# Batched self-attention with batch norm: which engine adds up three pairs of output groups, when segment rows are scaled, and the order of stores and loads in one queue

## The chip, the cores and the metric

The kernel runs on one core of a Trainium2 chip. The metric is the time of one execution on the device in microseconds; lower is better. The time of the kernel before is the median of three runs.

## The reference

There are 16384 tokens with 256 features (fp32), and each token belongs to one of 8 segments. Attention runs within a segment, over at most 3072 positions; a batch norm over all tokens follows, then a ReLU and a residual:

```python
q, k, v = feat @ Wq, feat @ Wk, feat @ Wv
starts = jnp.searchsorted(bids, jnp.arange(B))
pos = jnp.arange(N) - starts[bids]
qp, kp, vp = pad(q), pad(k), pad(v)          # zeros(B, 3072, .).at[bids, pos].set(x)
attn = softmax(where(mask, einsum('bld,bmd->blm', qp, kp), -1e9))
r = einsum('blm,bmd->bld', attn, vp)[bids, pos]
t = r @ Wt
tn = (t - t.mean(0)) / sqrt(t.var(0) + EPS) * gamma + beta
return feat + relu(tn)
```

The segment numbers are not sorted in these inputs. So most tokens have a position outside the 3072 places of their segment; their result is that of the segment's first or last place, one of 16 "edge rows". Only some 400 to 730 tokens of each segment own a place.

## The kernel before, in words

The function `fast_path` writes instructions for five engines through a small recorder (`pg`). Each engine carries out its instructions in the order in which they were recorded; the recorder puts in a semaphore wait wherever an operand asks for one. TensorE is PE, VectorE DVE, ScalarE ACT, GpSimd POOL; SP issues plain DMAs and computes nothing. SP's DMAs go through one queue, GpSimd's indirect DMAs through another, and both are carried by the same 16 DMA engines.

First come the attention of the eight segments, the sums for the batch norm, and the factors of the norm: these end at `y3` (line 1868), the normed edge rows after the ReLU in three bf16 parts. The change lies behind that, in the output stage (lines 1882 to 1949).

Three things are done there.

**Most tokens.** The tokens are cut into 16 groups of 1024 (1 MB each way), taken in the order `ORDER` (line 1056) and handled two at a time, as "pairs" `c` = 0 to 7 (lines 1897 to 1925). The features of a group are loaded by SP into one of nine buffers `fb` (`f0` to `f8`; `group_in`, line 1670), so load 9 reuses the buffer of group 0 and has to wait until store 0 has landed. Each group has four units of 128 x 512. For each, PE multiplies a one-hot matrix with `y3` into a PSUM bank. Then there are two ways to add the features:

- VectorE adds the bank to the unit in place (`pg.tt`, recorded at line 826), or
- PE also multiplies the unit by the identity into the same bank (line 1904), and ACT copies the bank over the unit (line 822).

`by_act` (line 1900) chooses: in pairs 1 to 7 ACT takes the units x = 4 and 6, VectorE x = 0 and 2. Seven PSUM banks are used in turn, so the eighth tile of a pair takes the bank of its first.

**Stores.** When a group's units are done SP issues its store (line 1920). Behind it stands, for groups from the third on, `finish` of the group two places earlier: SP waits for that store's landing and counts it in the semaphore `done` (line 1893). Then come loads for later groups, by the table `LATER`.

**Tokens that own a place.** Their rows lie in `tk`, up to six tiles of 128 rows for a segment. `rows(e)` (line 1882) scales, shifts, clips and adds the features on VectorE: two passes at line 826 that read the factors from PSUM, one at line 846 that reads two SBUF tiles. One segment is done after each pair. Rows that lose a place to another token (`tl`) are done last, by `normal` (line 1932). GpSimd then scatters the tiles into the output, one indirect DMA of 128 rows (131 KB) each (line 1939). These must overwrite what the plain stores wrote, so ahead of segment `e` GpSimd waits until `done` has reached the last group that the segment's tokens touch (line 1935). With these inputs the counts waited for are 3, 5, 5, 7, 7, 7, 11, 11 landings for segments 0 to 7, the tiles 4, 4, 5, 6, 6, 6, 4, 4; the closing `tl` scatters need 11 landings too.

Of the kernel before, what the change touches and what calls it, by code (L numbers as in the profile page):

```python
# [29 lines left out]
LT = 3  # L30
# [869 lines left out]
def fast_path(nc, feat, bids, wq, wk, wv, wt, gamma, beta, out, bad):  # L900
# [23 lines left out]
    def new(name, shape, dtype=F32):  # L924
        nonlocal end
        size = mybir.dt.size(dtype)
        for d in shape[1:]:
            size *= d
        plan.append((name, shape, dtype, end))
        h = at(name, shape, dtype, end)  # L930
        end += size + -size % 32
        return h
# [32 lines left out]
    xl, tl = new("xl", [P, LT, D]), new("tl", [P, LT, D])  # L965
# [253 lines left out]
    def present(e, t):  # L1219
        return ExitStack() if t < 4 else pg.given(e, t - 4)  # L1220
# [449 lines left out]
    def group_in(i, after=()):  # L1670
        pg.dma("SP", fb[i % NF][:], feat3[ORDER[i]], after)
# [108 lines left out]
    e = NB - 1  # L1780
# [58 lines left out]
    def unit(i, x):  # L1839
        return fb[i % NF][:, x : x + 2, :].rearrange("p t d -> p (t d)")  # L1840
# [29 lines left out]
    def normal(parts):  # L1870
        def over_t(s_, T):
            return norm[:, s_ * D : (s_ + 1) * D].unsqueeze(1).to_broadcast([P, T, D])

        for step in range(3):
            for when, y, x, T in parts:
                with when():
                    if step < 2:
                        pg.tt(y, y, over_t(step, T), (ALU.mult, ALU.add)[step])
                    else:
                        pg.stt(y, y, 0.0, x, ALU.max, ALU.add)  # L1880

    def rows(e):
        m = e * FT
        parts = [
            ((lambda lo=lo: present(e, lo)), tk[:, m + lo : m + hi, :], xs[:, m + lo : m + hi, :], hi - lo)
            for lo, hi in ((4, 5), (5, 6), (0, 4))
        ]
        normal(parts)
# [3 lines left out]
    def finish(w):  # L1892
        pg.op("SP", lambda e: e.sem_inc(done, 1), [], [], after=[w])  # L1893

    LATER = {5: (9, 10), 6: (11, 12), 7: (13,), 8: (14,), 9: (15,)}
    stores = []
    for c in range(NG // 2):
        pair = (2 * c, 2 * c + 1)
        for x in range(0, GT, 2):
            by_act = x >= 4 if c else x in (2, 4)  # L1900
            pf = [bank[(c * GT + x + r) % 7] for r in range(2)]
            if by_act and c:
                for r, i in enumerate(pair):
                    pg.mm(pf[r][:], ident[:], unit(i, x), start=True, stop=False)
            for u in range(2):
                for r, i in enumerate(pair):
                    h = slice(64 * r, 64 * r + 6 * NB)
                    pg.mm(
                        pf[r][:, u * D : (u + 1) * D], hot[h, c, x + u, :], y3[h, :],
                        start=not by_act, stop=True,  # L1910
                    )
            for r, i in enumerate(pair):
                if by_act:
                    pg.copy("ACT", unit(i, x), pf[r][:])
                else:
                    pg.tt(unit(i, x), unit(i, x), pf[r][:], ALU.add)
        for i in pair:
            f = fb[i % NF]
            stores.append(
                pg.op("SP", lambda e, i=i, f=f: e.dma_start(out3[ORDER[i]], f[:]), [f[:]], [], dma=True)  # L1920
            )
            if i >= 2:
                finish(stores[i - 2])
                for k_ in LATER.get(i, ()):
                    group_in(k_)
        rows(c)
        if c == 0:
            pg.ts(good[:], rdens[:], LIM, ALU.is_lt)
            pg.stt(good[:], rdens[:], 1.0 / LIM, good[:], ALU.is_gt, ALU.mult, accum=odd[:])
            pg.ts(odd[:], odd[:], -1.0, ALU.mult, float(TT), ALU.add)  # L1930
            pg.red(cnt_f[:, 0:1], over[:])
    normal([(ExitStack, tl[:], xl[:], LT)])

    for e in range(NB):
        pg.op("POOL", lambda x, e=e: (x.wait_ge(done, 1), x.wait_ge(done, pg.regs[("POOL", ("g", e))])), [], [])
# [30 lines left out]
def whole(nc, feat, bids, wq, wk, wv, wt, gamma, beta, out):  # L1966
    with nc.sbuf_tensor("bad", [P, 1], I32) as bad:
        regs, marks = fast_path(nc, feat, bids, wq, wk, wv, wt, gamma, beta, out, bad)
        engines = {"PE": nc.tensor, "ACT": nc.scalar, "DVE": nc.vector, "POOL": nc.gpsimd, "SP": nc.sync}
        for name, eng in engines.items():  # L1970
            eng.br_lt(regs[(name, "bad")], 1, on_true="all_done", on_false="any_lengths").branch_hint(marks[name])
        with nc.body("any_lengths", valid_engines=tuple(mybir.ALL_ENGINES)):
            nc.all_engine_barrier()
            with tile.TileContext(nc) as tc:
                any_lengths(tc, feat, bids, wq, wk, wv, wt, gamma, beta, out)
            nc.br("all_done")
        nc.switch_bb("all_done")
# [34 lines left out]
```

## Time and profile before

| | |
|---|---|
| median of three runs | 315.19 us (313.87 to 315.64) |
| profiled execution, its own time | 314.44 us |
| its span in the profile | 312.1 us |
| first store issued | 232.72 us |
| last scatter issued | 308.11 us |
| VectorE busy over the span | 225.7 us (72%) |
| PE, ACT, GpSimd busy | 252.1, 139.2, 126.8 us |
| DMA packets, mean rate | 56.84 MB, 182 GB/s |

The profile is one execution; times in it are microseconds from the start of the span. The engines' rows give start, duration, engine, line, operation, output<-inputs, sizes, how many were merged into the row ("x4"), and in brackets the idle time ahead of it with what ended it. A line is often that of a helper (826 is any addition of two tensors on VectorE), so the tiles' names tell more. SPq is SP issuing; a DMA takes longer than its issue, until it has landed.

### The profile page before, as it was taken

How to read it: one execution, taken by the hardware profiler on the slowest of the kernel's cores; microseconds unless marked ns; L12 is line 12 of the kernel's file. 1: busy time of each engine (PE TensorE's matmuls, PEld its weight loads, DVE VectorE, ACT ScalarE, POOL GpSimd, SP SyncE). 2: the span in 40 equal slices, each digit the busy share in tenths (PEclk: the TensorE clock that was granted, in tenths of full speed). 3: DMA queues.
4: the chain of work that ended last, by engine and by line, in shares of the span. 5: the costliest groups of instructions: out<-in, count | busy, mean ns of one | idle time of the engine just before them, and what ended most of it. 6: DMA issues, size and time to landing. Idle time of an engine off the chain costs nothing.

```text
span 312.1 us, 4505 instructions
## 1 busy us (share of the span) xinstructions
PE 252.1 (81%) x1206; PEld 168.3 (54%) x1206; DVE 225.7 (72%) x712; ACT 139.2 (45%) x298; POOL 126.8 (41%) x155
## 2 busy tenths in 40 slices
PE   1789788898798898999999999989977947675510
PEld 1656666665675777687878778757532212212100
DVE  7866778889979896736664765766389999794550
ACT  7345334367464628644754583574422311212110
POOL 3436580430430071006313753742221257677275
PEclk9998897999799999999999999999999995979585
DMA  3102069522222021112031330679997899999995
GB/s 98 35 24 64 6 200 345 174 68 70 67 67 70 34 70 29 67 61 81 26 95 36 90 101 17 196 274 377 326 391 322 355 351 404 424 417 413 420 417 204
DMA packets 23241, 56.84 MB, mean 182 GB/s; under 512 B 4768, under 2 KB 15858, under 8 KB 19114
## 3 DMA queue, kind: packets, MB, share of 16 engines
q1 hardware_dynamic: 17434, 45.77, 39.5%
q0 software_dynamic: 5232, 10.18, 10.1%
q10 hardware_dynamic: 544, 0.52, 0.5%
q8 instruction: 14, 0.23, 0.3%
q14 instruction: 17, 0.14, 0.1%
HBM read 26.73 MB, written 28.61 MB: 177 GB/s over the span
## 4 chain that ended last, share of the span: by engine, by line
PE 42%; DVE 26%; DMA 16%; ACT 7%; issue 6%; POOL 1%; POOLq 0%; DVEq 0%; SPq 0%; ACTq 0%
PE ps L807 39%; DMA out<-f 12%; DVE acc L846 4%; DMA f<-in_r_feat 4%; PE ps L812 2%; DVE junk L833 2%; DVE w L826 2%; DVE k L823 2%; ACT pa L817 1%; POOL out L892 1%; DVE ge L835 1%; DVE both L851 1%; ACT pb L817 1%; ACT sq L817 1%; ACT tk L817 1%
## 5 line engine op out<-in xcount | busy, mean ns | idle before, releaser
L882 POOL DMA_INDIRECT xs<-in_r_feat,idx x48 | 51.3, 1068 | 101.0 <-DVE idx L846 76.9
L807 PE MATMUL ps<-vs,pa 128*128 128x257 f32 x312 | 74.9, 389 | 4.7 <-ACT sq L817 3.6
L807 PEld LDWEIGHTS ps<-vs,pa 128*128 128x128 f32 x312 | 58.1, 193 | 16.8 <-ACT sq L817 4.8
L807 PE MATMUL ps<-f,ident 128*128 128x512 f32 x64 | 39.7, 733 | 20.1 <-DMA f<-in_r_feat 16.1
L892 POOL DMA_INDIRECT out<-tk,idx x39 | 40.0, 1027 | 31.3 <-SPq L1893 20.9
L817 ACT ACTIVATE tk<-ps,rdens 128x256 f32<-128x256 f32 x46 | 22.2, 483 | 62.5 <-DVE rdens L859 62.4
L822 ACT COPY f<-ps 128x512 f32<-128x512 f32 x32 | 17.1, 590 | 55.3 <-PE ps L807 55.3
L807 PE MATMUL ps<-wvt,xT 128*128 128x256 f32 x156 | 38.9, 400 | 0.3 <-DVE acc L846 0.3
L807 PEld LDWEIGHTS ps<-wvt,xT 128*128 128x128 f32 x156 | 30.6, 200 | 10.6 <-issue 4.1
L807 PEld LDWEIGHTS ps<-f,ident 128*128 128x128 f32 x64 | 12.2, 221 | 35.8 <-DMA f<-in_r_feat 19.6
L846 DVE SCALAR_TENSOR_TENSOR acc<-sq,reads_r,acc 128x256 f32<-128x256 f32 x45 | 21.6, 480 | 8.8 <-ACT sq L817 8.8
L826 DVE TENSOR_TENSOR f<-f,ps 128x512 f32<-128x512 f32 x32 | 20.1, 682 | 10.6 <-DMA f<-in_r_feat 10.0
L817 ACT ACTIVATE pa<-ps,mask 128x512 f32<-128x512 f32 x39 | 24.0, 690 | 7.5 <-PE ps L807 7.4
L826 DVE TENSOR_TENSOR tk<-tk,ps 128x1024 f32<-128x1024 f32 (+1 forms) x30 | 24.2, 843 | 0.3
L882 POOL DMA_INDIRECT reads_r<-reads_of,idx x12 | 13.4, 1119 | 24.8 <-ACT sq L817 11.8
L846 DVE SCALAR_TENSOR_TENSOR acc<-tk,reads_r,acc 128x256 f32<-128x256 f32 x45 | 21.5, 477 | 1.2 <-ACT tk L817 0.7
L807 PE MATMUL ps<-q,k 32*128 32x512 f32 (+2 forms) x154 | 20.6, 478 | 1.5 <-ACT pa L817 1.1
L823 DVE COPY k<-ps 32x128 f32<-32x128 f32 x40 | 11.8, 294 | 13.5 <-PE ps L807 12.6
L807 PE MATMUL ps<-xT,w 128*128 128x512 f32 (+1 forms) x60 | 20.6, 476 | 0.6 <-ACT xT L817 0.5
L807 PE MATMUL ps<-vs,pb 128*128 128x257 f32 x82 | 19.6, 387 | 0.0
L807 PEld LDWEIGHTS ps<-vs,pb 128*128 128x128 f32 x82 | 15.1, 189 | 6.5 <-issue 2.3
L817 ACT ACTIVATE q<-ps,cqk 96x512 f32<-96x512 f32 (+3 forms) x24 | 14.6, 608 | 7.8 <-PE ps L807 7.6
(260 smaller groups left out, 356.2 us busy)
## 6 DMA issues: line engine op xcount, KB each, us to landing
f<-in_r_feat SPq DMA_DIRECT2D x16, 1024.0 KB, 13.1
out<-f SPq DMA_DIRECT2D x16, 1024.0 KB, 10.1
t_rows<-tk SPq DMA_DIRECT2D x8, 512.0 KB, 3.9
xs<-zt SPq DMA_DIRECT2D x5, 768.0 KB, 10.4
t_rows<-tk SPq DMA_DIRECT2D x8, 256.0 KB, 2.5
eb<-edge_of SPq DMA_DIRECT2D x16, 96.0 KB, 2.3
xs<-in_r_feat,idx POOLq DMA_INDIRECT x48, 2.8
out<-tk,idx POOLq DMA_INDIRECT x39, 7.2
```

Of the source, the lines that this page charges most:

```text
L807: "PE", lambda e: e.matmul(out, lhsT, rhs, start=start, stop=stop, skip_group_check=True),
L812: return self.op("PE", lambda e: e.transpose(out, in_, ident), [in_, ident], [out])
L817: "ACT", lambda e: e.activation(out, in_, func, bias=bias, scale=scale), [in_, *more], [out]
L822: return self.op("ACT", lambda e: e.copy(out, in_), [in_], [out])
L823: return self.op(eng, lambda e: e.tensor_copy(out, in_), [in_], [out])
L826: return self.op(eng, lambda e: e.tensor_tensor(out, a, b, op), [a, b], [out])
L833: lambda e: e.tensor_scalar(out, a, s1, s2, op0, op1, accum_out=accum)
L835: else e.tensor_scalar(out, a, s1, s2, op0, op1),
L846: else e.scalar_tensor_tensor(out, a, s, b, op0, op1),
L851: return self.op("DVE", lambda e: e.tensor_reduce(out, in_, AX.X, op), [in_], [out])
L882: lambda e: e.indirect_dma_start(out=out, out_offset=None, in_=table, in_offset=bass.IndirectOffsetOnAxis(ap=ind, axis=0), bounds_check=n ...
L892: lambda e: e.indirect_dma_start(out=table, out_offset=bass.IndirectOffsetOnAxis(ap=ind, axis=0), in_=src, in_offset=None, bounds_check=n ...
```

## The change

Five things are changed, all in the output stage:

- In pairs 1 to 3 ACT takes only x = 6, and VectorE adds three units of each group instead of two.
- The rows of segments 0 to 3 are scaled one pair later, those of 4 and 5 after pair 5, those of 6 and 7 after pair 6.
- Both stores of a pair are issued first, and only then does SP wait for the landings of the pair before.
- The loads 9 to 12 come singly, one behind each counted landing.
- The `tl` rows are scaled ahead of pair 7 instead of last, and four short instructions on counts stand after pair 3 instead of pair 0.

```diff
-    LATER = {5: (9, 10), 6: (11, 12), 7: (13,), 8: (14,), 9: (15,)}
+    LATER = {3: (9,), 4: (10,), 5: (11,), 6: (12,), 7: (13,), 8: (14,), 9: (15,)}
+    ROWS = {1: (0,), 2: (1,), 3: (2,), 4: (3,), 5: (4, 5), 6: (6, 7)}
     stores = []
     for c in range(NG // 2):
         pair = (2 * c, 2 * c + 1)
         for x in range(0, GT, 2):
-            by_act = x >= 4 if c else x in (2, 4)
+            by_act = x >= (6 if c < 4 else 4) if c else x in (2, 4)
...
             stores.append(
                 pg.op("SP", lambda e, i=i, f=f: e.dma_start(out3[ORDER[i]], f[:]), [f[:]], [], dma=True)
             )
+        for i in pair:
             if i >= 2:
                 finish(stores[i - 2])
                 for k_ in LATER.get(i, ()):
                     group_in(k_)
-        rows(c)
-        if c == 0:
+        for e in ROWS.get(c, ()):
+            rows(e)
+        if c == 6:
+            normal([(ExitStack, tl[:], xl[:], LT)])
+        if c == 3:
             pg.ts(good[:], rdens[:], LIM, ALU.is_lt)
...
-    normal([(ExitStack, tl[:], xl[:], LT)])
```

SP's rows show what this does to its queue. Each row is an instruction; `out_0<-f3_79` is the store of the buffer `f3`, `f0_76<-in_r_feat` a load into `f0`, and in brackets stand the semaphores waited for: `of_SP_22` to `of_SP_25` are the landings of stores 0 to 3, `at_DVE` and `at_ACT` the engines that fill the buffer. Before, from the third store to the seventh:

```order
L1920 DMA out_0<-f2_78 128x2048 [waits at_DVE,at_ACT,of_SP_12]
L1920 DMA out_0<-f3_79 128x2048 [waits of_SP_22,at_DVE,at_ACT]
L1920 DMA out_0<-f4_80 128x2048 [waits of_SP_23,at_DVE,at_ACT,of_SP_15]
L1920 DMA out_0<-f5_81 128x2048 [waits of_SP_24,at_DVE,at_ACT]
L877 DMA f0_76<-in_r_feat 128x2048 [waits of_SP_25]
L877 DMA f1_77<-in_r_feat 128x2048
L1920 DMA out_0<-f6_82 128x2048 [waits at_DVE,at_ACT,of_SP_17]
```

The same place in the changed kernel:

```order
L1921 DMA out_0<-f2_78 128x2048 [waits at_DVE,at_ACT,of_SP_12]
L1921 DMA out_0<-f3_79 128x2048 [waits at_DVE,at_ACT]
L877 DMA f0_76<-in_r_feat 128x2048 [waits of_SP_22,of_SP_23]
L1921 DMA out_0<-f4_80 128x2048 [waits at_DVE,at_ACT,of_SP_15]
L1921 DMA out_0<-f5_81 128x2048 [waits at_DVE,at_ACT]
L877 DMA f1_77<-in_r_feat 128x2048 [waits of_SP_24]
L877 DMA f2_78<-in_r_feat 128x2048 [waits of_SP_25]
L1921 DMA out_0<-f6_82 128x2048 [waits at_DVE,at_ACT,of_SP_17]
```

The stores of a pair no longer wait for a landing in between; the first load stands ahead of the fifth store instead of behind the sixth, and the second, no longer beside the first, waits for a landing of its own.

On VectorE, `f2_78<-f2_78,ps1` adds a PSUM bank to a unit of group 2, and `tk_50<-tk_50,ps7` is a pass over the rows of a segment. This piece of the difference starts at the last additions of pair 0, after which the rows of segment 0 stood before:

```order
 L826 TENSOR_TENSOR f0_76<-f0_76,ps6 128x512
 L826 TENSOR_TENSOR f1_77<-f1_77,ps0 128x512
+L826 TENSOR_TENSOR f2_78<-f2_78,ps1 128x512
+L826 TENSOR_TENSOR f3_79<-f3_79,ps2 128x512
+L826 TENSOR_TENSOR f2_78<-f2_78,ps3 128x512
+L826 TENSOR_TENSOR f3_79<-f3_79,ps4 128x512
+L826 TENSOR_TENSOR f2_78<-f2_78,ps5 128x512
+L826 TENSOR_TENSOR f3_79<-f3_79,ps6 128x512
```

Pair 1's additions, six now, follow pair 0's at once, and the rows of segment 0 come behind them.

## The prediction

> **What bounds the kernel now.** I read four views: busy time by stretch, the timeline of the store queue, the chain of waits, and the timelines of GpSimd and VectorE. Only the last 85 of the 312.1 us concern the change; nothing ahead of the first store (232.72 us) is edited. First the stretches. The columns are the stretch, its length, busy us of PE, PEld, VectorE, ACT and GpSimd with counts, the granted clock, the busy share of the DMA engines, and GB/s:
>
> ```profile
> 236.00:246.00 10.00, 7.55 (x38) 2.45 (x36) 9.86 (x18) 3.09 (x7) 0.00 (x0) 1.00 0.84 342
> 246.00:256.00 10.00, 6.79 (x30) 2.21 (x30) 9.90 (x16) 2.90 (x6) 5.30 (x5) 1.00 0.90 323
> 266.00:276.00 10.00, 7.37 (x28) 2.60 (x26) 7.71 (x13) 2.71 (x6) 6.99 (x8) 0.83 1.02 421
> 286.00:296.00 10.00, 3.96 (x9) 1.36 (x10) 3.95 (x5) 1.07 (x2) 3.98 (x5) 0.66 1.01 414
> 296.00:306.00 10.00, 1.69 (x9) 0.57 (x7) 4.36 (x6) 1.07 (x2) 7.60 (x8) 0.81 1.01 414
> ```
>
> From 256 to 306 us the DMA engines are never free, while every compute engine is idle part of the time. Only between 236 and 256 us do they have room. Cut finer, the same view puts that room in two holes:
>
> ```profile
> 238.00:239.00 1.00, 0.84 (x2) 0.30 (x2) 1.00 (x3) 0.00 (x0) 0.00 (x0) 1.00 0.82 331
> 239.00:240.00 1.00, 0.87 (x11) 0.37 (x12) 1.00 (x3) 0.36 (x1) 0.00 (x0) 1.00 0.37 144
> 240.00:241.00 1.00, 1.00 (x6) 0.55 (x7) 1.00 (x1) 0.71 (x2) 0.00 (x0) 1.00 0.08 33
> 241.00:242.00 1.00, 1.00 (x3) 0.19 (x1) 0.97 (x2) 0.00 (x0) 0.00 (x0) 1.00 0.94 393
> 246.00:247.00 1.00, 1.00 (x6) 0.55 (x7) 1.00 (x2) 0.75 (x2) 0.00 (x0) 1.00 0.05 16
> 247.00:248.00 1.00, 1.00 (x4) 0.23 (x2) 0.97 (x3) 0.00 (x0) 0.37 (x1) 1.00 0.96 385
> ```
>
> The first hole is worth 0.18 + 0.63 + 0.92 + 0.06 = 1.79 us of all engines, the second 0.95 + 0.04 = 0.99 us: together **2.78 us**. The store queue's issues (start, length, "x2" for two) say why:
>
> ```profile
> 232.72 0.90 SPq L1920 DMA_DIRECT2D out<-f  x2
> 240.30 1.31 SPq L1920 DMA_DIRECT2D out<-f  x2
> 246.34 0.84 SPq L1920 DMA_DIRECT2D out<-f  x2
> 247.54 2.03 SPq L877 DMA_DIRECT2D f<-in_r_feat  x2
> ```
>
> Stores 0 and 1 are issued at 232.72 us, the next two only at 240.30, the next at 246.34, and no load stands in the queue before 247.54. Two stores of 1 MB keep the DMA engines for about 6 us (from 232.72 to the drop at 238.8), and each next pair comes later than that. I number stores s0 to s15 and loads l9 to l15 by their place in the order of groups.
>
> Now the end. The chain of waits (start, length) runs from load and store to store, and hands over to GpSimd; the last two rows are GpSimd's, and between them and the chain stands one store of SP with its time from issue to landing:
>
> ```profile
> 241.28 6.18 DMA out<-f
> 247.54 11.83 DMA f<-in_r_feat
> 266.32 15.26 DMA out<-f
> 281.73 16.79 DMA out<-f
> ...
> 275.80 0.82 SPq L1920 DMA_DIRECT2D out<-f  x1
> ...
> out<-f SPq DMA_DIRECT2D x1, 1024.0 KB, 19.6
> ...
> 296.27 0.99 POOL L892 DMA_INDIRECT out<-tk,idx  x1 [5.07 <-SPq L1893]
> 308.11 1.00 POOL L892 DMA_INDIRECT out<-tl,idx  x1 [0.30 <-issue]
> ```
>
> GpSimd idled 5.07 us until SP's count (line 1893) reached 11 stores: s10, issued at 275.80, landed 19.6 us later at 295.4. From 296.27 it issues the last ten scatters 1.3 us apart without a pause, to 308.11, and the span ends at 312.1. So the end is s10's landing plus about 16.7 us. s10 waits in a queue that is served in order; what decides is the DMA work ahead of it, and the holes in front.
>
> **The change part by part.** *SP's order.* SP's rows show store 3 waiting for landing 0 (of_SP_22), store 4 for landing 1 and store 5 for landing 2 before; afterwards each pair goes out first. Ahead of s10 stand s0 to s9 and l9 to l15 in both kernels, 17 MB, so s10 keeps its place. What moves inside: l9 from behind s5 to behind s3, l11 ahead of s6 instead of behind it, l14 behind s9. With SP free of landings, s2 is issued when its rows are added up, and that is VectorE's part:
>
> ```profile
> 230.77 2.48 DVE L826 TENSOR_TENSOR f<-f,ps 128x512 f32<-128x512 f32 x4 [0.55 <-PE ps L807]
> 233.17 2.47 DVE L826 TENSOR_TENSOR tk<-tk,ps 128x1024 f32<-128x1024 f32 x2
> 235.68 1.23 DVE L846 SCALAR_TENSOR_TENSOR tk<-tk,xs 128x1024 f32<-128x1024 f32 x1
> 261.20 3.79 DVE L826 TENSOR_TENSOR tk<-tk,ps 128x256 f32<-128x256 f32 x6
> 297.46 1.93 DVE L826 TENSOR_TENSOR tl<-tl,ps 128x768 f32<-128x768 f32 x2
> 299.53 0.96 DVE L846 SCALAR_TENSOR_TENSOR tl<-tl,xl 128x768 f32<-128x768 f32 x1
> 237.42 2.47 DVE L826 TENSOR_TENSOR f<-f,ps 128x512 f32<-128x512 f32 x4
> 239.64 1.07 ACT L822 COPY f<-ps 128x512 f32<-128x512 f32 x2 [3.02 <-PE ps L807]
> ```
>
> An addition takes 2.48 / 4 = 0.62 us; a segment of four tiles costs 2.47 + 1.23 = 3.7 us, one of six 3.79 + 1.90 = 5.7 us (the 1.90 in a row further down), the closing rows 1.93 + 0.96, with gaps 3.0 us. Pairs 1 to 3 give VectorE six additions instead of four: 6 more, 6 x 0.62 = **3.7 us more on VectorE**, and take two ACT copies (1.07 us) and two identity matmuls off each pair. Pair 1 now follows pair 0 at once: 233.25 + 6 x 0.62 = 237.0, store 2 about 0.6 us sooner. ACT's last copies hang on the bank that VectorE's first addition frees; they ended at 239.64 + 1.07 = 240.7 before, 3.3 us after that addition began at 237.42, so now at 236.5, under VectorE's additions. That is before 239, when the first hole opens: the hole closes. Rows 0 then run to 240.7, pair 2 to 244.4, so s4 and s5 go out 1.9 us earlier than 246.34; and l9, released when s1 has landed (about 241), already stands between. The second hole closes too. Sum of the two: -2.78 us. Nothing else is free to be filled until s10.
>
> *Is VectorE late afterwards?* Adding on: rows 1 to 248.1, pair 3 to 251.9, rows 2 (five tiles, 4.8) to 256.7, the counts moved to pair 3 0.6, pair 4 to 259.8, rows 3 to 265.5, pair 5 to 268.0, rows 4 and 5 to 279.5, pair 6 to 282.0, rows 6 and 7 to 289.4, closing rows to 292.4, pair 7 to 294.9. s14 can't be issued before s11 has landed, 281.73 + 16.79 - 2.78 = 295.7. So VectorE is ahead, and the queue still holds s12 and s13 then. The closing rows cost nothing where they go: VectorE idled there for loads, and GpSimd wants them last.
>
> *GpSimd's other waits:*
>
> ```profile
> 247.63 1.02 POOL L892 DMA_INDIRECT out<-tk,idx  x1 [12.45 <-SPq L1893]
> 254.78 0.98 POOL L892 DMA_INDIRECT out<-tk,idx  x1 [1.92 <-SPq L1893]
> 267.57 0.99 POOL L892 DMA_INDIRECT out<-tk,idx  x1 [1.19 <-SPq L1893]
> 276.60 1.59 POOL L892 DMA_INDIRECT out<-tk,idx  x1 [0.30 <-issue]
> 290.21 0.99 POOL L892 DMA_INDIRECT out<-tk,idx  x1 [0.30 <-issue]
> 275.44 1.90 DVE L846 SCALAR_TENSOR_TENSOR tk<-tk,xs 128x256 f32<-128x256 f32 x3
> ...
> 248.00:260.00 12.00, 5.38 (x24) 1.94 (x24) 11.83 (x18) 2.15 (x4) 8.08 (x8) 0.91 1.00 358
> 262.00:284.00 22.00, 17.58 (x66) 6.25 (x64) 18.97 (x27) 5.68 (x11) 16.24 (x17) 0.78 1.02 422
> ```
>
> The third wait, at 267.57, is for the seventh landing, s6. That one now has l11 in front of it as well. Scatters take 131 KB / 1.3 us = 101 GB/s of the 422, which leaves 321, so one more MB costs 3.3 us; less 2.78 that is 268.1. From there the 18 scatters of segments 3 to 5, the last issued at 290.21, kept GpSimd until 291.5 before, so now until 292.0. s10's landing releases GpSimd at 296.27 - 2.78 = 293.5. **GpSimd's spare time shrinks from 5.07 to about 1.5 us** but stays positive, and the end moves by the full 2.78. Rows 3 (265.5), 4 (273.7 against 276.0) and 5 (279.5 against 284) are ready in time.
>
> One scatter at 276.60 took 1.59 us, beside VectorE's last pass over a segment (275.44, 1.90 us), 0.6 us more than the usual 0.99. The Trainium skill's page "SBUF — State Buffer", section "Who interferes with whom", has a rule that speaks against this change: a VectorE instruction with two SBUF inputs, as that pass is, contends with a GpSimd instruction that reads SBUF, and the loser blocks fully. By that rule alone each pass that runs under the scatters, seven or eight now, could cost GpSimd the whole pass. The row gives 0.6 us at worst, once; with one segment more under the scatters than before I take nothing, and put 0 to 0.6 us into the range.
>
> *The rate.* 358 GB/s between 248 and 260 us against 422 later, at a full busy share: 12 x (1 - 358/422) = 1.8 us are lost there, and the profile doesn't say to what. I take it as unchanged; the bounds are that it goes (-1.8) or doubles (+1.8).
>
> **Sum.** The profiled execution took 314.44 us, 2.34 around its span of 312.1. 314.44 - 2.78 = 311.7. It lay 0.75 below the median of the three runs, 315.19; against the median the forecast is 315.19 - 2.78 = **312.4 us**. A run of this kernel can tell about 0.5%, 1.6 us, from no change.
>
> **The rivals.** *GpSimd takes over.* If s6 lands some 3 us later than 268.1 (l11 is in front of it), or several passes stretch the scatters by 0.6 us, the 18 scatters end at about 295 instead of 292.0. Then GpSimd starts the last ten scatters at 295 instead of 293.5; 1.5 us of the gain go, 1.3 remain: 313.9, which can't be told from no change. For it: the slow stretch lies just ahead of s6. Against: s6 needs only the MBs counted, and a wait of 1.19 us was all GpSimd had there.
>
> *Loads among stores slow the DMA engines (slower).* Loads now mix with stores from 241 us on, and l9 to l15 are in the queue until about 286. If the mixing is what made 248 to 260 slow, 358 instead of 422 GB/s could hold from 244 to 286: 42 x (1 - 358/422) = 6.4 us, less the 1.8 paid now and the 2.78 gained, +1.8 and so 317.0. It decides where the mean rate over these 42 us falls under 422 x (1 - 4.6/42) = 376 GB/s. Against: 262 to 284 holds loads and stores mixed too, at 422.
>
> *VectorE becomes the bound.*
>
> ```profile
> DVE f L826 <- DMA f<-in_r_feat: 10.0, 4, 6.7
> ```
>
> VectorE is busy 9.86 and 9.90 of 10 us in the stage, and gets 3.7 us more. If all that follows hung on it, the end would come 3.7 later: 318.9. For that, rows 4 would have to miss 276.0 by more than GpSimd's 1.5 us, which is VectorE 3.8 us later than reckoned. Against: after this stage it waited for loads four times, 10.0 us in all, and that absorbs the 3.7. The Trainium skill's page "Perfetto Trace Analysis", section "Identifying the Most-Contended Engine", has the engine of highest occupancy optimized first and takes occupancy as a fair measure for the Vector engine; by that rule this stage is VectorE's, loading it further is wrong, and the time would be that 318.9.
>
> **How the numbers follow.** Both holes close, end follows: 0.66. GpSimd takes over, or the rate eats half: 0.20. Loads slow the stores: 0.09. VectorE: 0.05. The first case spans 310.6 (the slow stretch gone) to 314.2. Of its 0.66 some 0.06 end within 0.5%: faster 0.61 with a little from the second case, same 0.28, slower 0.11. The range for 8 in 10 is 310.6 to 315.6.
>
> **What would show it.** Right: no slice under a 0.9 DMA share between 234 and 300 us, stores 2 and 3 issued near 237, l9 near 241, GpSimd's wait for s10 under 2 us, released near 293.5. Wrong: a hole left near 239 or 246 (VectorE or ACT late), scatters from 268 to 292 with no wait after them (GpSimd bound), or a rate under 400 GB/s after 262 (mixing).

## The result, and the profile after

The changed kernel takes **312.27 us** (median of 21 runs), the kernel before 314.43 us (21 runs beside them): ratio **0.9947**, 95% interval 0.9929 to 0.9965, so 1.7 us less. (The ratio leaves out a slow run of the kernel before, 603.88 us; the medians alone differ by 2.2 us.) A second comparison (`e0_after`) gave 311.52 against 314.09, ratio 0.9907, 0.9873 to 0.9941, so 2.9 us less. Predicted were 312.4 us and a ratio of (315.19 - 2.78) / 315.19 = 0.9912. The forecast was right in sign and about in size; that the time itself fits to 0.1 us is luck, since the kernel before was now measured 0.76 us lower than the 315.19 it started from. The places it named in the store queue were right as well. How closed holes turn into time at the end was not, as the experiments show.

The profiled execution took 313.69 us, 1.4 above its own median, with a span of 311.4 us; so I read places and mechanisms from it, and sizes from `e0_after` as well (311.16 us, span 308.8).

The stretches of 10 us in the changed kernel; the columns are those of the prediction's first fence:

```profile
236.00:246.00 10.00, 7.68 (x40) 2.47 (x38) 9.90 (x13) 2.15 (x4) 0.43 (x1) 0.84 1.02 400
246.00:256.00 10.00, 8.03 (x25) 2.66 (x24) 9.90 (x15) 2.15 (x4) 5.14 (x5) 0.65 1.01 393
286.00:296.00 10.00, 7.29 (x11) 2.31 (x12) 7.39 (x9) 1.07 (x2) 6.74 (x7) 0.56 1.02 424
296.00:306.00 10.00, 2.01 (x8) 0.43 (x6) 0.16 (x1) 1.07 (x2) 7.57 (x9) 0.67 0.90 355
```

The DMA share from 236 to 256 us was 0.84 and 0.90 and is 1.02 and 1.01: the room is gone. But the stretch from 296 to 306, full before (1.01), now has room (0.90). Cut to single microseconds:

```profile
239.00:240.00 1.00, 0.46 (x2) 0.00 (x0) 0.97 (x2) 0.00 (x0) 0.00 (x0) 1.00 1.05 423
240.00:241.00 1.00, 0.00 (x0) 0.00 (x0) 1.00 (x3) 0.00 (x0) 0.00 (x0) 1.00 1.05 442
244.00:245.00 1.00, 1.00 (x6) 0.56 (x6) 1.00 (x1) 0.00 (x0) 0.00 (x0) 0.50 0.76 197
246.00:247.00 1.00, 0.64 (x1) 0.00 (x0) 0.97 (x2) 0.00 (x0) 0.69 (x2) 0.50 1.12 328
297.00:298.00 1.00, 0.62 (x5) 0.13 (x4) 0.00 (x0) 0.34 (x1) 0.70 (x2) 0.76 0.69 277
```

At 239 to 241 stood 0.37 and 0.08 before, at 246 0.05. All three are full. What is new: a dip at 297 (three slices of 0.72, 0.69 and 0.67), and a stretch of low rate from 243 to 249 (326 GB/s at a mean share of 1.00, the slice at 244 being down to 0.76), where before the low rate lay at 248 to 260. So the sign "no slice under 0.9 between 234 and 300" did not come out. The store queue:

```profile
232.62 6.46 SPq L1921 DMA_DIRECT2D out<-f  x4
241.40 0.34 SPq L877 DMA_DIRECT2D f<-in_r_feat  x1
243.46 1.15 SPq L1921 DMA_DIRECT2D out<-f  x2
244.73 2.02 SPq L877 DMA_DIRECT2D f<-in_r_feat  x2
```

The first row now holds four stores in 6.46 us: the third was issued at 237.8 (predicted 237.0, before 240.30), l9 at 241.4 (predicted 241), s4 at 243.46 (predicted 244.4, before 246.34). And GpSimd, first where it waits for s10, then two scatters and the VectorE pass beside the second:

```profile
292.37 0.98 POOL L892 DMA_INDIRECT out<-tk,idx  x1 [0.30 <-issue]
295.09 0.98 POOL L892 DMA_INDIRECT out<-tk,idx  x1 [1.74 <-SPq L1893]
...
262.32 0.99 POOL L892 DMA_INDIRECT out<-tk,idx  x1 [0.30 <-issue]
263.61 1.94 POOL L892 DMA_INDIRECT out<-tk,idx  x1 [0.30 <-issue]
...
262.79 1.90 DVE L846 SCALAR_TENSOR_TENSOR tk<-tk,xs 128x256 f32<-128x256 f32 x3
```

Its idle time ahead of the last ten scatters shrank from 5.07 to 1.74 us; about 1.5 was predicted. The scatter at 263.61 took 1.94 us where 0.99 is usual; it ended 0.86 us after the VectorE pass beside it (262.79 + 1.90 = 264.69). More on that below.

### The profile page after: what moved, and what is told of

The parts are those of the page before. It is cut to its first block, busy times and chain, and to the rows that moved or that the text cites. A ratio compares the mean times of both kernels' runs of the same rounds, so it can differ in the third digit from the quotient of the medians.

```text
span 311.4 us, 4481 instructions
## 1 busy us (share of the span) xinstructions
PE 252.2 (81%) x1194; PEld 166.8 (54%) x1194; DVE 229.3 (74%) x718; ACT 135.8 (44%) x292; POOL 129.7 (42%) x155
## 4 chain that ended last, share of the span: by engine, by line
PE 39%; DVE 30%; DMA 14%; ACT 7%; issue 6%; POOL 2%; DVEq 1%; SPq 0%; POOLq 0%; ACTq 0%
PE ps L807 37%; DMA out<-f 14%; DVE acc L846 4%; DVE f L826 3%; DVE w L826 2%; DVE junk L833 2%; PE ps L812 2%; DVE k L823 2%; DVE tk L826 2%; POOL out L892 2%; ACT pa L817 1%; DVE ge L835 1%; ACT xT L817 1%; ACT tk L817 1%; DVE both L851 1%
## 5 line engine op out<-in xcount | busy, mean ns | idle before, releaser
L807 PE MATMUL ps<-vs,pa 128*128 128x257 f32 x312 | 73.6, 384 | 4.7 <-ACT sq L817 3.6
L807 PEld LDWEIGHTS ps<-vs,pa 128*128 128x128 f32 x312 | 57.1, 189 | 16.5 <-ACT sq L817 4.8
L807 PE MATMUL ps<-f,ident 128*128 128x512 f32 x52 | 38.3, 855 | 19.6 <-DMA f<-in_r_feat 14.4
L892 POOL DMA_INDIRECT out<-tk,idx x39 | 42.9, 1100 | 26.8 <-DVE tk L826 10.4
L807 PE MATMUL ps<-wvt,xT 128*128 128x256 f32 x156 | 39.6, 405 | 0.3 <-ACT pa L817 0.3
L822 ACT COPY f<-ps 128x512 f32<-128x512 f32 x26 | 13.9, 590 | 58.9 <-PE ps L807 58.9
L826 DVE TENSOR_TENSOR f<-f,ps 128x512 f32<-128x512 f32 x38 | 23.3, 681 | 0.6 <-PE ps L807 0.6
```

Of the source, the lines that this page charges most:

```text
L807: "PE", lambda e: e.matmul(out, lhsT, rhs, start=start, stop=stop, skip_group_check=True),
L822: return self.op("ACT", lambda e: e.copy(out, in_), [in_], [out])
L826: return self.op(eng, lambda e: e.tensor_tensor(out, a, b, op), [a, b], [out])
L892: lambda e: e.indirect_dma_start(out=table, out_offset=bass.IndirectOffsetOnAxis(ap=ind, axis=0), in_=src, in_offset=None, bounds_check=n ...
```

## The experiments

The first store came at 231.6 to 237.9 us in the profiles of these runs, though nothing ahead of it is edited, and a ratio mixes that in. So beside each ratio stands the *stage*: the span less the start of the first store, both from the run's profile (before: 312.1 - 232.72 = 79.4). "Hole 1" and "hole 2" are what the DMA share falls short of 1, summed over the first 14 slices of 1 us after the first store, and over the next 14. They aren't quite the two holes of the prediction: the first slice or two, while the queue fills, fall 0.2 to 0.9 us short in every run, and in the kernel before the edge at 14 us cuts the second hole in two.

| kernel | ratio, 95% | stage, us | third store after the first, us | hole 1 | hole 2 |
|---|---|---|---|---|---|
| before | | 79.4 | 7.6 | 2.8 | 0.8 |
| changed | 0.9947 (0.9929 to 0.9965) | 78.8 | 5.2 | 1.1 | 0.3 |
| e0_after | 0.9907 (0.9873 to 0.9941) | 77.2 | 5.4 | 0.7 | 0.3 |
| e1_sp_only | 0.9981 (0.9953 to 1.0008) | 78.4 | 7.6 | 2.5 | 0.3 |
| e2_compute_only | 0.9925 (0.9890 to 0.9960) | 77.2 | 5.4 | 1.1 | 0.4 |
| e3_tail | 0.9925 (0.9890 to 0.9960) | 78.5 | 3.8 | 0.6 | 0.3 |
| e4_rows0_first | 0.9971 (0.9929 to 1.0013) | 79.3 | 8.3 | 2.9 | 0.4 |
| e5_rows01_first | 1.0120 (1.0066 to 1.0175) | 83.3 | 11.9 | 7.0 | 0.3 |
| e6_rows_only | 0.9934 (0.9891 to 0.9977) | 80.9 | 7.3 | 2.4 | 0.6 |
| e7_no_first_scatters | 0.9832 (0.9769 to 0.9896) | 74.6 | 5.4 | 0.8 | 0.5 |
| e8_rows_alone | 0.9911 (0.9875 to 0.9948) | 77.3 | 7.3 | 2.5 | 0.5 |
| e9_adds_alone | 1.0222 (1.0161 to 1.0282) | 86.2 | 8.9 | 3.6 | 2.5 |
| e10_late_loads | 1.0018 (0.9984 to 1.0053) | 80.3 | 5.4 | 0.6 | 0.3 |
| e11_rows_pair1 | 0.9835 (0.9774 to 0.9895) | 76.5 | 5.4 | 0.6 | 0.4 |

The profiled executions of the changed kernel, e2, e3, e5 and e6 lay 1.0 to 1.7 us above the median of their own runs, that of e10 1.2 below; the others within 0.8.

**The change again, and its two halves.** `e0_after` is the changed kernel. `e1_sp_only` is the kernel before with SP's new order alone, `e2_compute_only` the changed kernel with SP's old order:

```diff
 e1_sp_only, against before
-    LATER = {5: (9, 10), 6: (11, 12), 7: (13,), 8: (14,), 9: (15,)}
+    LATER = {3: (9,), 4: (10,), 5: (11,), 6: (12,), 7: (13,), 8: (14,), 9: (15,)}
...
+        for i in pair:
             if i >= 2:
                 finish(stores[i - 2])
...
 e2_compute_only, against the changed kernel: these lines taken back
```

> The changed kernel once more, to stand beside the others on one chip: about 2.1 us under the kernel before (medians so far 314.43 and 312.27), ratio 0.993 to 0.995. Its profile should again have no hole between 236 and 243 us, and s10's landing (GpSimd's release) 1 to 3 us ahead of 296.27.

> Only SP's order is changed (both stores first, loads singly); additions and rows as before. Theory of the holes: s2 is still issued near 240.3, since VectorE scales the rows of segment 0 first, so the first hole (1.79 us) stays; l9 now stands behind s3, so the second (0.99 us) closes: 1.0 us gained, 313.4, ratio 0.997. Rival, the waits for landings are what held the queue: nearly the whole gain, 2.0 us, 312.4.

> Only the engines' part (three units on VectorE, rows later); SP issues store, landing, loads as before. Theory of the holes: s2 goes out near 237.8, s4 and s5 near 244 to 246, before s2 and s3 are through; both holes close and the gain is that of the whole change, about 2.1 us: 312.3. Rival, the waits for landings held the queue: s3 waits for landing 0 and s5 for landing 2, so the holes stay and nothing is gained, 314.4.

The 13 us that hold both holes, in the kernel before, in e1 and in e2, one row of each:

```profile
236.00:249.00 13.00, 10.55 (x49) 3.63 (x48) 12.83 (x21) 4.14 (x9) 1.06 (x2) 1.00 0.80 325
```

```profile
236.00:249.00 13.00, 12.10 (x55) 3.86 (x54) 12.81 (x21) 4.29 (x8) 0.56 (x1) 0.98 0.85 320
```

```profile
236.00:249.00 13.00, 9.66 (x41) 2.78 (x39) 12.86 (x17) 2.15 (x4) 3.16 (x4) 0.76 1.02 425
```

The shares are 0.80, 0.85 and 1.02. SP's order alone closes the second hole and leaves the first; its ratio can't be told from 1. The new order of the computing engines closes both, with SP as it was. So SP's half adds nothing that these runs can tell.

**Holes put back, one and two.** In the changed kernel the rows of segment 0 go back to pair 0 (e4), and then those of segment 1 with them (e5):

```diff
 e4_rows0_first
-    ROWS = {1: (0,), 2: (1,), 3: (2,), 4: (3,), 5: (4, 5), 6: (6, 7)}
+    ROWS = {0: (0,), 2: (1,), 3: (2,), 4: (3,), 5: (4, 5), 6: (6, 7)}
 e5_rows01_first
+    ROWS = {0: (0, 1), 3: (2,), 4: (3,), 5: (4, 5), 6: (6, 7)}
```

> The changed kernel with the rows of segment 0 scaled ahead of pair 1 again (as before); all else as changed. Theory of the holes: VectorE reaches pair 1 some 3.7 us later, s2 goes out near 241 and the DMA engines run dry at 239.5; the first hole is back, 1.0 to 1.8 us, and the time is that much above the changed kernel's 311.5 to 312.3: about 313.5. Rival, the gain comes from SP's order and the second hole: no more than 0.5 above the changed kernel.

> As the one before, with the rows of segment 1 ahead of pair 1 too: s2 another 3.7 us later, near 244.7, a hole of 4.7 to 5.5 us. Theory of the holes: the end follows one to one, 3.7 us above the run before, about 317. Rival, the work behind has slack that takes up a late start of the stores: 314 or less.

The same 13 us in e4 and in e5, one row of each:

```profile
236.00:249.00 13.00, 11.06 (x38) 3.96 (x40) 12.62 (x18) 1.29 (x3) 1.25 (x2) 0.50 0.81 320
```

```profile
236.00:249.00 13.00, 6.82 (x32) 2.10 (x30) 12.86 (x16) 2.05 (x4) 2.66 (x3) 0.58 0.59 239
```

With segment 0 ahead the hole is back (0.81), and by the stage (79.3) the gain is gone; the ratio alone, whose interval reaches from 0.9929 to 1.0013, can't tell e4 from the changed kernel. With segment 1 ahead too, hole 1 is 7.0 - 2.9 = 4.1 us longer (the rows overstate it, since e5's first store came 2.3 us later than e4's), the stage 83.3 - 79.3 = 4.0 us, and the time 321.81 - 317.36 = 4.45 us: here a hole costs its own length at the end.

**Is the end DMA work?** `e7_no_first_scatters` leaves out 12 scatters (tiles 0 to 3 of segments 0 to 2 are not written, and the count of writes that the end waits for is 12 lower), 1.57 MB or 3.7 us at 422 GB/s:

```diff
-        for t in range(FT):
+        for t in range(4 if e < 3 else 0, FT):
```

> The changed kernel without 12 of the 41 scatters (the four constant tiles of segments 0, 1 and 2 are not written to the output). Theory that the DMA work ahead of s10 sets the end: 12 x 131 KB at 422 GB/s is 3.7 us less, so about 3.7 us under the changed kernel, 308.3. Rival, GpSimd's chain of scatters sets it, and its second half starts only with the landing of s6 and of s10 whatever came first: if those landings don't move, under 1 us.

It took 312.63 us where the kernel before took 319.19 and e6 (below), on the same chip, 316.55. Its stage is 77.2 - 74.6 = 2.6 us shorter than that of e0: most of the 3.7, but not all. But the edit takes work from GpSimd as well as from the DMA engines, so it can't tell the two theories apart. In its trace GpSimd waits for VectorE, whose pass over segment 3 ended at 267.73, and from there it issues 28 scatters without a pause, so without waiting for s10 (its first and last row):

```profile
268.62 1.00 POOL L892 DMA_INDIRECT out<-tk,idx  x1 [7.70 <-DVE f L826]
305.69 0.98 POOL L892 DMA_INDIRECT out<-tl,idx  x1 [0.30 <-issue]
```

**The dip at 297.** In the profile of the changed kernel the last two stores (298.3) waited for ACT's copies of pair 7, which the prediction had forgotten when it let VectorE's additions end that pair:

```profile
293.49 1.07 ACT L822 COPY f<-ps 128x512 f32<-128x512 f32 x2 [10.29 <-PE ps L807]
297.66 1.07 ACT L822 COPY f<-ps 128x512 f32<-128x512 f32 x2 [3.10 <-PE ps L807]
```

`e3_tail` gives three of that pair's four steps to VectorE and lets SP issue s14 ahead of the landings:

```diff
-            by_act = x >= (6 if c < 4 else 4) if c else x in (2, 4)
+            by_act = x >= (4 if 4 <= c < 7 else 6) if c else x in (2, 4)
...
-        for i in pair:
+        for i in pair if c < 6 else (12,) if c == 6 else (13, 14, 15):
```

> The changed kernel, but in pair 7 ACT takes only x = 6 as well, and the landing of s11 is counted behind the issue of s14 and s15. In the changed kernel's profile the DMA engines are at a share of 0.72, 0.69 and 0.67 from 296 to 299 us, 0.9 us lost, because s14 is issued only at 298.3. Theory that this tail takes back part of the gain: s14 goes out near 296, the dip is gone, and 0.5 to 1.0 us are gained on the changed kernel, about 311.5. Rival, GpSimd's chain of the last ten scatters behind s10 alone sets the end: nothing, 312.3.

s14 went out at 295.4, 2.9 us earlier than in the changed kernel's profile, and nothing was gained (312.35 us, on a chip where e0 took 311.52). The dip itself went: from 296 to 302 us the slices hold a share of 0.94 to 1.07. It is also missing in the profile of e0, the changed kernel itself, where s14 went out at 295.2. So the dip goes with the late s14 of that one execution. But filling it gains nothing: the share is a mean over 16 engines, and in e3 it only falls sooner at the end (0.69 at 303, where the changed kernel has 1.01). The slowest engines decide (last section).

**Rows, additions, and one without the other.** e6 is the changed kernel with `by_act` as before; e8 is the kernel before with the rows, the closing rows and the counts moved and nothing else; e9 is the kernel before with the additions alone:

```diff
 e6_rows_only, against the changed kernel
-            by_act = x >= (6 if c < 4 else 4) if c else x in (2, 4)
+            by_act = x >= 4 if c else x in (2, 4)
 e8_rows_alone, against before
+    ROWS = {1: (0,), 2: (1,), 3: (2,), 4: (3,), 5: (4, 5), 6: (6, 7)}
...
-        rows(c)
+        for e in ROWS.get(c, ()):
+            rows(e)
...
 e9_adds_alone, against before
-            by_act = x >= 4 if c else x in (2, 4)
+            by_act = x >= (6 if c < 4 else 4) if c else x in (2, 4)
```

> The changed kernel with the additions as before: ACT takes x = 4 and 6 in pairs 1 to 3. Theory: it is the later rows that let pair 1 out before the stores run dry; ACT's four copies and PE's four identity matmuls take pair 1 to 237 to 239, so no hole comes back: the changed kernel's time within 0.7 us, 311.5 to 312.7. Rival, the shift to VectorE is needed because PE, at half its clock in some of this stretch, holds up ACT: s2 at 240 or later and 1.0 to 1.8 us lost, about 313.5.

> The kernel before with only the later rows (and the closing rows and counts moved): additions and SP's order as before. Theory of the holes: the rows that stood between pair 0 and pair 1 alone made s2 late; without them it goes out at 237 to 239 and the ratio is that of the whole change, 0.991 to 0.995. Rival, all three parts are needed together: 0.997 or more.

> The kernel before with only the additions of pairs 1 to 3 moved to VectorE; rows and SP's order as before. Theory of the holes: VectorE still scales rows 0 ahead of pair 1 and now adds six times instead of four, so s2 goes out at 240.3 to 241 and both holes stay or grow by up to 0.6 us: ratio 1.000 to 1.003. Rival, ACT and PE were what held pairs 1 to 3: s2 earlier than 239.5 and a ratio under 0.997.

The additions alone cost 7.6 us, where 0 to 1 was expected. In e9 VectorE does pair 0, rows 0, six additions, rows 1, six additions and so on, with 1.2 us more in each of the pairs 1 to 3; and the rows of segments 6 and 7 still stand behind pairs 6 and 7. Its second hole is 2.5 us instead of 0.8, and later the rows of its PE, ACT, VectorE and GpSimd read:

```profile
279.42 0.83 PE L807 MATMUL ps<-y,hot 48*128 48x256 bf16 x12
...
291.24 1.07 ACT L822 COPY f<-ps 128x512 f32<-128x512 f32 x2 [10.71 <-remote]
...
296.24 0.69 DVE L826 TENSOR_TENSOR f<-f,ps 128x512 f32<-128x512 f32 x1 [13.11 <-remote]
...
306.90 0.98 POOL L892 DMA_INDIRECT out<-tk,idx  x1 [8.74 <-DVE f L826]
```

VectorE waited 13.11 us for pair 6, the rows of segment 6 stand behind that pair, and GpSimd waited 8.74 us for them. ("remote" means that the trace doesn't show what released it. ACT's last copies of pair 5 came at 291.24, though PE's matmuls for them, among the twelve of the first row, were over at 280.25; what held them is open. PE's own next row stands only at 291.94, so the delay may be PE's as much as ACT's.) The two holes of e9 are 3.6 + 2.5 - 2.8 - 0.8 = 2.5 us longer than before; the rest of the loss hangs in this profile on those late copies. So the additions cost nothing that shows where the rows stand behind them (e0, e2) and hurt where they don't (e9); that the order alone is the reason is argued, not shown.

The rows alone (e8) give the whole gain: 0.9911, stage 77.3. e6's ratio, 0.9934, agrees; its stage of 80.9 comes from a profile with a stall of its own (see below). But the way is not the prediction's, for in e8 the first hole is still there:

```profile
236.00:238.00 2.00, 2.00 (x4) 0.68 (x2) 2.00 (x5) 0.00 (x0) 0.29 (x1) 0.51 1.08 442
238.00:240.00 2.00, 2.00 (x8) 0.53 (x7) 1.97 (x3) 0.47 (x1) 0.00 (x0) 0.64 1.00 418
240.00:242.00 2.00, 2.00 (x16) 0.80 (x14) 1.66 (x2) 0.88 (x3) 0.00 (x0) 1.00 0.54 217
242.00:244.00 2.00, 2.00 (x10) 0.71 (x8) 1.98 (x4) 0.80 (x2) 0.00 (x0) 1.00 0.47 197
```

PE is busy every microsecond: with ACT's two steps in pair 1, PE's identity matmuls, not VectorE, keep s2 until 242.4, 7.3 us after the first store. The granted clock is part of it: 0.51 and 0.64 in the first two rows, where the kernel before had 1.00, and the first four identity matmuls took 3.32 us instead of 1.96. In e6 it was the same (s2 at 242.0, clock 0.50): there the rival came true in its first half, and its loss of 1.0 to 1.8 us did not. So the additions do close the first hole, by freeing PE; e0 and e2, with the hole closed, still end no sooner than e8 without it.

What e8 gains is therefore for the most part not a hole. By s10's landing its DMA engines had carried 23.04 MB since the first store, in the kernel before 24.15: 1.1 MB less, an estimated 2.6 us at 422 GB/s, and s10 landed 3.5 us sooner. 0.6 MB of it are scatters (3.23 against 3.83 MB), the rest plain transfers: the faster engines had run less far ahead of the slowest one. No run tries why. The question for the next run was where the hole's 1.8 us go.

**One pair's additions.** `e11_rows_pair1` is e8 with the additions in pair 1 alone:

```diff
-            by_act = x >= 4 if c else x in (2, 4)
+            by_act = x >= (6 if c == 1 else 4) if c else x in (2, 4)
```

> The rows are scaled later as in the changed kernel, SP's order is the one of before, and VectorE takes over ACT's units x = 4 in pair 1 alone (two additions instead of six). With the rows alone, stores 2 and 3 were still issued 7.3 us after the first store and the DMA engines idled 2.5 us of the next 14 (2.8 before). Both theories expect stores 2 and 3 about 5.4 us after the first store here, as in the changed kernel, and under 1.2 us of idle time in those 14 us. Theory one, a hole's length is gained at the end: then the time falls by another 1.5 us or so against the rows alone, ratio to the kernel before 0.984 to 0.988, and 75.5 to 76 us from the first store to the end. Theory two, what sets the end is no longer the holes but GpSimd's forty scatters and the slowest DMA engine: s10 lands up to 1.5 us sooner, GpSimd or the last stores give it back, 77.0 to 77.5 us from the first store to the end, ratio 0.990 to 0.993 as with the rows alone.

The hole closed (0.6 us, third store 5.4 us after the first), the stage is 76.5: 0.8 us of 1.9 came through, between the two theories. The ratio, 0.9835, is the best of the kernels that write everything, and its interval ends below that of the changed kernel (0.9895 against 0.9929). The runs of the kernel before spread widely on that chip (318 to 322.4), so the better measure is the stage, 0.7 below e0's. GpSimd's rows of e11, the first scatter, the three later ones with a named releaser, and the first of the last ten:

```profile
247.63 1.02 POOL L892 DMA_INDIRECT out<-tk,idx  x1 [10.83 <-DVE tk L826]
267.40 0.98 POOL L892 DMA_INDIRECT out<-tk,idx  x1 [2.05 <-DVE f L826]
277.56 0.98 POOL L892 DMA_INDIRECT out<-tk,idx  x1 [2.74 <-DVE tk L846]
289.59 0.99 POOL L892 DMA_INDIRECT out<-tk,idx  x1 [0.30 <-DVE tk L826]
295.53 0.98 POOL L892 DMA_INDIRECT out<-tk,idx  x1 [1.09 <-issue]
```

The last row names no releaser, but it is the wait for s10: the last of s10's recorded increments is at 294.66, 0.87 us earlier, and in the kernel before, the changed kernel, e0 and e2 the first of the last ten scatters starts 0.87 us after s10's landing too. So GpSimd waited for s10 in e11 (1.09 us), as in e0 and e2 (0.98 and 1.17), and only in e8 did it come too late to have to. Up to there it had issued 31 scatters at 1.29 us, waited twice for VectorE's rows, and been held up as below.

What differs is what comes behind s10. From s10's landing to the last scatter's issue it is 12.5 us in the changed kernel, e0, e2 and e11 (12.7 before): GpSimd, once released, loses nothing. From that issue to the end it is 3.95 us before, 4.7 in the changed kernel, 5.1 in e0, 5.7 in e2 and 5.2 in e11. There the last store and the last scatters land later behind their issue, and that is where a part of the closed hole went.

**The loads later.** `e10_late_loads` is the changed kernel with l13 to l15 behind s11, so that s10 has 3 MB less ahead of it:

```diff
-    LATER = {3: (9,), 4: (10,), 5: (11,), 6: (12,), 7: (13,), 8: (14,), 9: (15,)}
+    LATER = {3: (9,), 4: (10,), 5: (11,), 6: (12,), 10: (13,), 11: (14,), 12: (15,)}
```

(and rows 6 and 7 after pair 5, the closing rows after pair 7, three of four steps of pairs 6 and 7 on VectorE; SP counts s10 ahead of s12 instead of behind s13).

> A version that the theory points to: the changed kernel with loads 13 to 15 behind s10 and s11 instead of ahead of them, rows 4 to 7 all after pair 5, the closing rows after pair 7, three units on VectorE in pairs 6 and 7 too. Theory that the end is GpSimd's last ten scatters behind s10's landing, plus 16 to 17 us: s10 has 14 MB ahead of it instead of 17 and lands near 282 instead of 294, GpSimd then runs from the landing of s6 to its end without a wait, 28 scatters of 1.3 us, about 302.5 instead of 306.7, and 2 to 3 us are gained on the changed kernel: about 309.5, ratio 0.985. Rival, the total of DMA work and its slowest engine set the end: s15 lands no earlier than 309, and nothing or a loss of up to 2 us comes of it, since pairs 6 and 7 now wait longer for their loads.

Ratio 1.0018. s10 counted at 284.2, but VectorE now waits for the loads of the last pairs:

```profile
292.87 3.08 DVE L826 TENSOR_TENSOR f<-f,ps 128x512 f32<-128x512 f32 x5 [4.74 <-DMA f<-in_r_feat]
299.71 1.88 DVE L826 TENSOR_TENSOR f<-f,ps 128x512 f32<-128x512 f32 x3 [2.74 <-DMA f<-in_r_feat]
```

The closing rows came at 306.7 and the last scatter at 311.4: the wait only moved. (The closing scatters began at 310.06, 3.3 us after their rows. Ahead of them the program has GpSimd read a value that VectorE wrote at 308.0, behind ACT's last copies; the trace names no releaser for either.)

## Why the prediction was right, and where not

- **The DMA engines bound the stage; holes are what can be gained.** Held in part. e4 against e5 prices a hole that is put in at its own length (4.1 and 4.0 us). A hole that is closed gave less (e11: 0.8 of 1.9), and e8 gained as much as e0 with the first hole open. That the forecast of 2.78 us lies near the measured 1.7 and 2.9 is therefore luck in part.
- **s2 at 237, l9 at 241, s4 at 244.4; both holes close.** Held (237.8, 241.4, 243.46). But ACT's copies did not finish under VectorE's additions at 236.5. VectorE's additions of pairs 0 and 1, and ACT's last copies of pair 1:

```profile
230.67 6.07 DVE L826 TENSOR_TENSOR f<-f,ps 128x512 f32<-128x512 f32 x10 [0.55 <-PE ps L807]
237.15 1.07 ACT L822 COPY f<-ps 128x512 f32<-128x512 f32 x2 [4.21 <-PE ps L807]
```

  VectorE was done at 236.74, ACT at 238.22, so ACT's two copies came last ahead of s2 and s3. They waited for PE: at a granted clock of 0.50 its four identity matmuls took 3.21 us, against 1.96 in the kernel before at 1.00. In e0 it is the same (235.75 and 237.48). The prediction carried over a time measured at full clock; that it didn't matter is luck, since the DMA engines had s1 to carry until 241.3.
- **VectorE's 3.7 us lie beside the path.** Held for the changed kernel (it was done with pair 7 at 293.6, predicted 294.9). e9 shows a case where they don't: there the rows had not moved. The rival "VectorE becomes the bound" (318.9) fell: VectorE was at 9.9 of 10 us before and after, and the time fell. The Trainium skill's page "Perfetto Trace Analysis", section "Identifying the Most-Contended Engine", has the engine of highest occupancy optimized first, and has DMA judged by its use of HBM instead; going by VectorE's occupancy alone, as that rival did, was wrong here.
- **SP's order.** I gave it a share in both holes. e1 and e2 give it the second hole at most, and nothing beyond the computing engines' order.
- **GpSimd's spare shrinks to about 1.5 us.** 1.74 measured, by luck: GpSimd was done with segment 5 at 293.35 (predicted 292.0) and released at 295.09 (predicted 293.5), 1.4 and 1.6 us late. I took nothing for the passes of VectorE that hold up scatters, with 0.6 us as the bound. Summed over the scatters that took over 1.1 us, what they took beyond 0.99 is 1.3 us before, 4.4 in the changed kernel, 4.7 in e0: **3 us more**. What hid the error is that the wait for s6 (1.19 us before) was gone, since s6 landed at 266.2, and that s10 landed later than forecast. The first scatter's earlier start (245.57 instead of 247.63) did not help: GpSimd then waited 3.94 us for the fifth landing, 1.92 before, and went on at 255.03 instead of 254.78.
- **"The end moves by the full 2.78"** is the step that was mis-sized. Against the first store, s10's landing moved by 62.7 - 61.6 = 1.1 us in the changed kernel's profile and by 3.1 in e0, the end by 0.6 and 2.2; and "the end is s10's landing plus 16.7" is no constant: 17.1, in e0 17.6, in e2 18.2, in e8 18.1. As the times under e11 show, in the changed kernel, e0 and e2 the difference lies behind the last scatter's issue. The rival "GpSimd takes over" forecast 1.3 us of gain, near the measured 1.7 but not the 2.9 of e0; its mechanism, GpSimd too late for s10, did not occur in either profile.
- **The slow stretch** stayed, as assumed, but moved: 358 GB/s at 248 to 260 before; in the changed kernel the six slices from 243 to 249 fall 1.4 us short of 422 GB/s, in e0 1.5 us, with 0.4 us of missing share. It goes with the first load: in all 14 profiles the first slice under 300 GB/s that isn't a hole begins 2 to 5 us after l9 is issued, whether l9 goes out 7.5 or 17 us after the first store, and in e7 it begins 13 us ahead of the first scatter. Its cause is open.
- **Loads among stores slow the DMA engines** (317.0): fell as a lasting effect; what may be due to loads is the short stretch above. In e0, with l10 to l12 among the stores from 249 us on, the rate (last column) stays far above the 376 GB/s from which that rival would decide:

```profile
249.00:261.00 12.00, 9.25 (x39) 3.33 (x38) 11.83 (x24) 3.22 (x6) 7.80 (x7) 0.84 1.02 424
261.00:295.00 34.00, 21.92 (x62) 6.64 (x62) 30.92 (x43) 5.84 (x11) 26.01 (x25) 0.70 1.01 414
```

What stays open: why e8's slowest DMA engine was less far behind at s10 than before, which of the 16 DMA engines fall behind and why, what lowers the rate behind the first load, and what held ACT or PE in e9. (In e6's profile ACT also stood idle, 24 us to 297.29, without a releaser that the trace names.)

## What to carry to other kernels

Where a queue of transfers is the bound, look for the stretches in which it ran dry and ask which engine's order made it wait; moving work that nobody waits for behind the work that feeds the queue can be worth more than making either faster. Then ask what ends last once the hole is closed: a hole put in cost its length here, a hole closed did not give it back in full. A contention that had been priced at one row took 3 us of GpSimd's 5 us to spare. Adding load to an engine and reordering it are two edits: test them apart, since one can hurt without the other.

## What the runs showed of the hardware that I had not expected

**A scatter is held until the VectorE pass ends.** The pass at line 846 reads two SBUF tiles; three pairs in the changed kernel, the scatter first:

```profile
246.90 1.60 POOL L892 DMA_INDIRECT out<-tk,idx  x1 [0.30 <-issue]
255.03 1.82 POOL L892 DMA_INDIRECT out<-tk,idx  x1 [3.94 <-SPq L1893]
283.55 1.86 POOL L892 DMA_INDIRECT out<-tk,idx  x1 [0.30 <-issue]
...
246.39 1.22 DVE L846 SCALAR_TENSOR_TENSOR tk<-tk,xs 128x1024 f32<-128x1024 f32 x1
254.36 1.62 DVE L846 SCALAR_TENSOR_TENSOR tk<-tk,xs 128x256 f32<-128x256 f32 x2
283.32 1.23 DVE L846 SCALAR_TENSOR_TENSOR tk<-tk,xs 128x1024 f32<-128x1024 f32 x1
```

The passes end at 247.61, 255.98 and 284.55, the scatters at 248.50, 256.85 and 285.41: 0.86 to 0.89 us later each time, whenever they began. So do all scatters over 1.05 us in the kernel before, the changed kernel, e0, e8 and e11. It is as if a scatter that begins inside the pass started only when the pass ends. The Trainium skill's page "SBUF — State Buffer", section "Who interferes with whom", has a VectorE instruction with two SBUF inputs contend with a GpSimd instruction that reads SBUF, and calls the ports they share an exclusive lock; these ends agree with it. The prediction knew the rule and took the smaller row. It matters who comes first: a scatter that was already under way when the next pass began was not held, and this one, which began 0.04 us after its pass, took its usual time while the pass took 1.29 us instead of 1.22:

```profile
287.00 0.98 POOL L892 DMA_INDIRECT out<-tk,idx  x1 [0.30 <-issue]
...
286.96 1.29 DVE L846 SCALAR_TENSOR_TENSOR tk<-tk,xs 128x1024 f32<-128x1024 f32 x1
```

**A store lands when the slowest of its 16 shares has.** The trace holds a time for each of a store's 16 increments. First, eighth and last:

```
            s2                     s6                     s10                    s15
before      244.0  244.1  244.6    263.6  263.8  266.3    291.1  292.0  295.4    305.8  306.5  310.4
changed     242.1  242.4  243.8    262.0  262.5  266.2    287.0  288.5  294.2    305.1  305.3  309.9
e0_after    240.8  241.0  241.8    261.4  261.8  264.1    286.6  287.1  291.2    302.0  302.9  307.4
```

They land 0.6 to 1.7 us apart at s2 and 4.3 to 7.2 us apart at s10 (2.5 in e8). The eighth share of s10 came 3.5 us sooner in the changed kernel, the last, which alone releases GpSimd, 1.2. That the increments come from engines that finish independently is stated by the Trainium skill's page "DMA: Bandwidth & Descriptors", section "Why a DMA increments its semaphore by 16 and not by 1"; that the lag grows over 60 us of full load is what these runs add. It is a reason why a mean DMA share overstates a hole: in the kernel before the laggards still worked on s1 until 241.1, inside the first hole. And it fits the dip at 297 in the changed kernel: by 297.9 eight shares of s13 had landed and had no store behind them until s14 at 298.3, while the slowest share of s12 landed at 300.3. Both steps are argued from these times; no run tried them by themselves.
